# Row sums carried by the neighbour product, and the last block's output product among the first scores

## The chip, the cores and the metric

One Trainium2 chip, of which the kernel uses one core. The metric is the device time of one execution in microseconds (us). TensorE is written PE in the profile (its weight loads PEld), VectorE is DVE, ScalarE is ACT, GpSimd is POOL, and SP issues most DMAs.

## The reference

One layer of a graph network, followed by attention and a mixture of experts, for 4096 tokens of 256 channels, all in float32. Only the first part matters here:

```python
h   = features @ neigh_W.T              # features = layernorm(x) over the 256 channels
deg = adj.sum(axis=1, keepdims=True) + 1.0
h   = adj @ h / deg                     # adj is 4096 x 4096
z   = concatenate([features, h], axis=-1) @ lin_W.T
x   = x + z
```

Then `x = x + ffn(layernorm(x))`, in which `ffn` is causal attention with 4 query heads and 2 key heads of 64 channels, a router to the best 2 of 8 experts, and gated experts. Two facts are used below. A layer-normed row has no gain or offset here, so its 256 channels add up to zero: each channel is minus the sum of the other 255. And `deg` is the row sum of `adj`, which is what `adj` times a column of ones gives.

## The kernel before, in words

**Folding.** `neigh_W` and the second half of `lin_W` are multiplied once at the start into one 256x256 matrix `m_sb` (`fold`, L359 to L367), so the neighbour part is `(adj @ features) @ m / deg`. PE first runs 26 transposes of an identity into an unused bank (`idle`, L657 to L659) and goes on to `fold` when they are done.

**Neighbour product.** The tokens are cut into 8 blocks `b` of 512 rows, and `adj` into 8 x 8 pieces, one 1 MB DMA for each (`load`, L244). `aggregate(b)` (L492) walks over 8 column pieces `jb` and adds each piece's product with the normed features `g[jb]` into four PSUM banks, `acc`. It uses Strassen's scheme: seven products of half size in place of eight. The sums of quarters of `adj` that this needs are made on DVE by `halve` (L448: S1, S2, S4, S3, L459 to L462); the last of them is written in place over a quarter of the piece. The sums of quarters of the features are made once by `halve_x` (L421). Features are normed by `normed_x` (L409, DVE), turned by `turned_x` (L416, PE transposes at L397, ACT copies at L399) and multiplied by the first half of `lin_W` in `features` (L476, PE at L485). All this is done in the first pass, block 0, in between its eight pieces; PE reaches `tr` of block 3 in its second piece.

**Order inside a pass.** The order is written by hand: `steps[jb]` is a list of functions called after the fourth of the seven products of piece `jb`, and `steps[jb, "end"]` after the seventh. In pass `b` (from 1 on) these steps are the query, key and value work of block `b-1` (`qkv`, L580): scales, norm, turn, values, key heads and query heads, at pieces 1 to 6. The heads are rotated by ACT (L638) and POOL (L642, L643). At the end of a pass ACT copies product 1 out of its bank (L522) and DVE adds the seven products up (L523 to L525, L531 to L534) into `neighbours`, which lies in the room of `kT[7]` and `vv[7]`.

**Degrees.** POOL adds the sums S4 and S1 of the eight pieces up into `all_s` (L467 to L474). At the end of the pass PE multiplies `all_s` by ones: four products of 32 columns each, at four column positions of the array (`sums`, L544); ACT copies the result (L550). In the first piece of the next pass PE turns it (`degrees`, L554), DVE adds 1 and inverts it (L556, L559), and `linear` (L561) multiplies `neighbours` by `m_sb` (L566) and adds the result, divided by the degrees, to `res[b]` (DVE, L573). For the last block there is no next pass: `degrees` and `linear` run at once, ahead of attention.

**Attention's start.** Blocks come in `ORDER` 3, 0, 4, 1, 5, 2, 6, 7; the unit of work is a key tile `s` for a pair of heads. `scores` (L792) is 16 PE instructions into one of two double banks (`p_sc0`, `p_sc2`), then an exponential on ACT (L809). `totals` (L818, DVE L829) adds the probabilities up, `values` (L833, PE L843) multiplies them by V. Seven scores are issued ahead of the first values. Other work is placed among the units by number: the first in the list is `last_qkv` (L1150), the query, key and value work of block 7, which reads `res[7]`: statistics on DVE (L159), powers on POOL (L165, L166), norm on DVE (L174), transposes on PE (L1171). DVE runs in program order, so these statistics come after the totals of units 1 to 5.

**PSUM.** In the first part the banks are `g_tr` 0 and 1, `g_pj` 2 and 3, `acc` 4 to 7. In attention `y_third` has 0, `ms` 1, `p_sc1` (`y_first`, `y_second`) 2 and 3, `p_sc0` 4 and 5, `p_sc2` 6 and 7.

Of the kernel before, what the change touches and what calls it, by code (L numbers as in the profile page):

```python
# [9 lines left out]
F32 = mybir.dt.float32  # L10
# [7 lines left out]
P = 128  # L18
# [48 lines left out]
def fast_kernel(  # L67
# [114 lines left out]

    def ratio(pool, b):
# [45 lines left out]
    with (  # L229
# [28 lines left out]
        m_sb = gw.tile([P, 2, C], F32, name="m_sb")  # L258
        l1_sb = qT[6][:, :, 0:C]
        nc.scalar.dma_start(l1_sb, lin_t[0:C, :].rearrange("(c p) o -> p c o", p=P))  # L260
        for n in range(2):
            load_x(1 + n)
            load(n)
# [95 lines left out]
        def fold():  # L359
            for c in range(2):  # L360
                pm = p_pj.tile([P, 512], F32, tag="pj", name=f"pm_{c}")
                for k in range(2):
                    nc.tensor.matmul(
                        pm[:, :C], wn_sb[:, k, c * P : (c + 1) * P], l2_sb[:, k, :],
                        start=(k == 0), stop=(k == 1),
                    )
                nc.scalar.copy(m_sb[:, c, :], pm[:, :C])  # L367
# [53 lines left out]
        def halve_x(b):  # L421

            part = [g[b][:, k] for k in range(7)]
            nc.vector.tensor_sub(part[T1], part[G12], part[G11])
            nc.vector.tensor_sub(part[T3], part[G22], part[G12])
            nc.vector.tensor_sub(part[T2], part[G22], part[T1])
            nc.vector.tensor_sub(part[T4], part[T2], part[G21])
# [13 lines left out]
        neighbours = [  # L441
            kT[NB - 1].rearrange("p (r i) -> p r i", r=2),
            vv[NB - 1].rearrange("p (r t) c -> p r (t c)", r=2),
        ]

        all_s = gs.tile([P, 2, 2, 2 * P], F32, name="all_s")

        def halve(n):  # L448

            if n == NB * NB:  # L450
                return
            a = blocks.pop(n)
            m = {
                f"A{r + 1}{k + 1}": a[:, 2 * k : 2 * k + 2, r * 2 * P : (r + 1) * 2 * P]
                for r in range(2) for k in range(2)
            }
            m["S1"], m["S2"], m["S4"] = sums_at[n % 2]
            m["S3"] = m["A21"]
# [5 lines left out]
            jb = n % NB  # L464
# [71 lines left out]
        def finish(b):  # L536

            made = {}

            def sums():  # L540

                tr = p_tr.tile([P, 2, 2, P], F32, tag="tr", name=f"degT_{b}")
                for t in range(TB):
                    nc.tensor.matmul(  # L544
                        tr[32 * t : 32 * (t + 1), 0, 0, :], ones[:, 0:32],
                        all_s[:, t // 2, 0, t % 2 * P : (t % 2 + 1) * P],
                        start=True, stop=True, skip_group_check=True, tile_position=(0, 32 * t),
                    )
                made["degT"] = gx.tile([P, P], F32, tag="degT", name=f"degs_{b}", bufs=1)
                nc.scalar.copy(made["degT"], tr[:, 0, 0, :])  # L550

            def degrees():
                tr = p_tr.tile([P, 2, 2, P], F32, tag="tr", name=f"deg_{b}")
                nc.tensor.transpose(tr[:, 0, 0, :], made["degT"], ident)  # L554
                deg = made["deg"] = gx.tile([P, TB], F32, tag="deg", name=f"degr_{b}", bufs=1)
                nc.vector.tensor_scalar_add(  # L556
                    deg, tr[:, 0, 0, :].rearrange("p (t i) -> p t i", i=32)[:, :, 0], 1.0
                )
                nc.vector.reciprocal(deg, deg)  # L559

            def linear():  # L561
                for r in range(2):
                    pj = p_pj.tile([P, 2, C], F32, tag="pj", name=f"ph_{b}_{r}")
                    for t in range(2):
                        for c in range(2):
                            nc.tensor.matmul(  # L566
                                pj[:, t, :], neighbours[c][:, r, t * P : (t + 1) * P],
                                m_sb[:, c, :], start=(c == 0), stop=(c == 1),
                            )
                    for t in range(2):  # L570
                        i = 2 * r + t
                        x1 = res[b][:, i, :]
                        nc.vector.scalar_tensor_tensor(  # L573
                            x1, pj[:, t, :], made["deg"][:, i : i + 1], x1,
                            op0=ALU.mult, op1=ALU.add,
                        )

            return sums, degrees, linear

        def qkv(b):  # L580
# [26 lines left out]
            def values_and_logits():  # L607
                for h in range(2):
                    pj = p_pj.tile([P, 2, C], F32, tag="pj", name=f"pv_{b}_{h}")
# [15 lines left out]
            def turned_heads(ms):  # L625
# [21 lines left out]
                [values_and_logits], [lambda: turned_heads((2,))],  # L647
                [lambda: turned_heads((0, 1))],
# [16 lines left out]
        turned_x(0)  # L665
        features(0)
# [21 lines left out]
        for b in range(NB):  # L688
            sums, degrees, linear = finish(b)
# [6 lines left out]
            steps[NB - 1, "end"] = [sums]  # L696
# [8 lines left out]
    with (  # L705
# [8 lines left out]
        p_sc1, p_sc0, p_sc2 = (  # L714
            sc_scope.enter_context(tc.tile_pool(name=f"a_sc{n}", bufs=bufs, space=PSUM))
            for n, bufs in ((1, 2), (0, 1), (2, 1))
# [496 lines left out]


# [1455 lines left out]
```

## Time and profile before

| what | value |
|---|---|
| median of 3 runs | 1541.57 us (1540.42 to 1542.78) |
| the profiled execution, its own time | 1539.6 us |
| its span in the profile | 1537.9 us |
| outside the span | 1.7 us |
| granted PE clock over the span | 0.998 |
| first neighbour product starts | 18.45 us |
| one pass of `aggregate` with its steps (passes 1 to 7) | 60.35 us |
| attention's first score | 525.07 us |
| POOL busy with `all_s`, the form that names `more_sums` | 101.5 us in 72 instructions |

The pass time is the distance of the PE rows of L544 from pass to pass (218.33, 278.68, 339.02, 399.37). A row of a timeline has the start, the length, the engine, the line, the operation, out and in by name, the shape and the number of instructions in it; in brackets stands the idle time of the engine just before, and what ended it. PE's rows overlap by a fraction of a us, [...]so the cost of PE work is read from start to start. A float32 product with 256 columns is two PE instructions and 0.433 us from start to start (8 of them at L514 take 1.73 us).

### The profile page before, as it was taken

The page shows a single profiled execution, that of the slowest core. Times are in us where ns is not written, and L with a number is a line of the kernel's source. Part 1 is how long each engine was busy: PE and PEld are TensorE (multiplying, and loading weights), DVE is VectorE, ACT ScalarE, POOL GpSimd, SP SyncE. Part 2 cuts the span into 40 slices and gives each one's busy share as a digit, 9 for nine tenths or more (in the row PEclk, how much of TensorE's full clock was granted, in tenths as well). Part 3 has the DMA queues.
Part 4 walks back from the last instruction along what each step waited for, and adds up shares of the span by engine and source line. Part 5 has one row for each costly group of instructions (what it writes and reads, how often), then busy time and mean ns, then how long its engine had stood idle before and what let it go on. Part 6 is the DMA issues. An engine that isn't in the chain of part 4 may idle for free.

```text
span 1537.9 us, 28358 instructions
## 1 busy us (share of the span) xinstructions
PE 1524.7 (99%) x10995; PEld 1125.1 (73%) x10995; DVE 1075.4 (70%) x2150; ACT 555.4 (36%) x986; POOL 717.3 (47%) x730
## 2 busy tenths in 40 slices
PE   9999999999999999999999999999999999999998
PEld 7888888888888543444444444458899999999997
DVE  8965655756656467779879879794565777677762
ACT  1101121121120456555656656553122333343331
POOL 3435545554655422364564563442424455455442
PEclk9999999999999999999999999999999999999999
DMA  6334544444445000011010111038766877787855
GB/s 239 128 119 149 174 141 147 151 140 148 153 138 161 22 1 16 29 40 44 33 57 28 34 40 31 28 127 328 225 208 199 263 227 255 240 254 256 270 142 135
DMA packets 69520, 212.16 MB, mean 138 GB/s; under 512 B 17824, under 2 KB 45856, under 8 KB 55744
## 3 DMA queue, kind: packets, MB, share of 16 engines
q1 hardware_dynamic: 56112, 192.25, 36.6%
q0 software_dynamic: 12720, 17.47, 5.7%
q8 instruction: 89, 1.46, 0.4%
q10 hardware_dynamic: 544, 0.52, 0.1%
q14 instruction: 55, 0.45, 0.1%
HBM read 184.48 MB, written 27.13 MB: 138 GB/s over the span
## 4 chain that ended last, share of the span: by engine, by line
PE 94%; DVE 3%; POOL 1%; issue 1%; ACT 1%; DMA 0%; POOLq 0%; DVEq 0%; ACTq 0%
PE acc L514 23%; PE sc L801 15%; PE h L1713 13%; PE y_first L843 5%; PE y_second L843 5%; PE ye_y L1769 5%; PE y_third L843 4%; PE hA L1540 4%; PE ye_y L1670 3%; PE ye_ms L1670 2%; PE pq L629 2%; PE ph L566 2%; PE hD L1540 2%; PE pf L485 1%; PE po L920 1%; PE tx L1428 1%
## 5 line engine op out<-in xcount | busy, mean ns | idle before, releaser
L801 PE MATMUL sc<-qT_all,kT 64*64 64x512 f32 (+3 forms) x2304 | 281.9, 557 | 0.9 <-ACT pt_all L809 0.5
L514 PE MATMUL acc<-a,g 128*128 128x256 f32 x1024 | 245.9, 380 | 0.0
L514 PEld LDWEIGHTS acc<-a,g 128*128 128x128 f32 x1024 | 192.4, 190 | 32.4 <-issue 6.7
L801 PEld LDWEIGHTS sc<-qT_all,kT 64*64 64x64 f32 x2304 | 91.2, 133 | 129.9 <-issue 108.2
L809 ACT ACTIVATE pt_all<-sc 128x1024 f32<-128x1024 f32 (+3 forms) x157 | 149.0, 956 | 95.5 <-PE sc L801 94.9
L469 POOL TENSOR_TENSOR all_s<-all_s,more_sums 128x512 f32<-128x512 f32 x72 | 101.5, 1423 | 120.4 <-DVE more_sums L461 120.4
L1791 POOL DMA_INDIRECT acc_dram<-y,late x40 | 63.2, 1580 | 180.6 <-ACT y L1780 92.4
L514 PE MATMUL acc<-more_sums,g 128*128 128x256 f32 x512 | 126.3, 379 | 0.0
L829 DVE TENSOR_TENSOR late<-late,pt_all 128x1024 f32<-128x1024 f32 (+3 forms) x92 | 106.7, 1160 | 23.1 <-ACT pt_all L809 11.3
L514 PEld LDWEIGHTS acc<-more_sums,g 128*128 128x128 f32 x512 | 97.2, 190 | 13.2
L1713 PE MATMUL h<-late,qT_all 128*128 128x256 f32 (+1 forms) x616 | 105.2, 327 | 0.0
L843 PE MATMUL y_second<-pt_all,vv 64*64 64x512 f32 (+3 forms) x440 | 105.0, 555 | 0.0
L843 PE MATMUL y_first<-pt_all,vv 64*64 64x512 f32 (+3 forms) x440 | 104.3, 553 | 0.0
L1713 PEld LDWEIGHTS h<-late,qT_all 128*128 128x128 f32 x616 | 94.0, 191 | 9.6 <-ACT late L1434 0.8
L399 ACT COPY qT_all<-tr 128x512 f32<-128x512 f32 x30 | 16.2, 589 | 234.7 <-PE tr L397 234.6
L1079 POOL DMA_INDIRECT lists<-row,slots x64 | 89.8, 1402 | 17.9 <-issue 15.2
L638 ACT ACTIVATE rot<-pq 32x512 f32<-32x512 f32 x84 | 49.5, 589 | 120.4 <-DVE kT L636 55.0
L1720 DVE TENSOR_TENSOR late<-si,h 128x256 f32<-128x256 f32 (+2 forms) x87 | 39.9, 467 | 74.4 <-ACT si L1719 43.7
L843 PE MATMUL y_third<-pt_all,vv 64*64 64x512 f32 (+3 forms) x376 | 89.8, 557 | 0.0
L1719 ACT ACTIVATE si<-h 128x256 f32<-128x256 f32 (+2 forms) x87 | 36.5, 421 | 145.1 <-PE h L1713 138.6
L811 POOL TENSOR_SCALAR_AFFINE_SELECT pt_all<-pt_all 128x256 f32<-128x256 f32 x36 | 19.4, 542 | 109.7 <-ACT pt_all L809 82.1
L1713 PE MATMUL h<-late,pt_all 128*128 128x128 f32 (+1 forms) x440 | 65.7, 306 | 0.0
(479 smaller groups left out, 3471.5 us busy)
## 6 DMA issues: line engine op xcount, KB each, us to landing
a<-in_adj_dram SPq DMA_DIRECT2D x64, 1024.0 KB, 5.0
qT_all<-in_w_dram SPq DMA_DIRECT2D x18, 1408.0 KB, 8.4
pt_all<-in_w_dram SPq DMA_DIRECT2D x16, 1408.0 KB, 8.5
res_all<-in_w_dram SPq DMA_DIRECT2D x17, 768.0 KB, 5.1
pt_all<-in_w_dram SPq DMA_DIRECT2D x16, 768.0 KB, 5.0
res_all<-in_w_dram SPq DMA_DIRECT2D x8, 1408.0 KB, 8.2
qT_all<-in_w_dram SPq DMA_DIRECT2D x9, 768.0 KB, 4.4
late<-lists SPq DMA_DIRECT2D x25, 265.0 KB, 2.9
```

Of the source, the lines that this page charges most:

```text
L469: nc.gpsimd.tensor_add(all_s[:, i], all_s[:, i], sums_at[n % 2][k])
L514: nc.tensor.matmul(acc[bank][:, at, :], g[jb][:, right, k, :], m[left][:, k, :], start=(jb == 0 and k == 0 and at == 0), stop=(jb == NB - ...
L801: nc.tensor.matmul(ps[k * HP : (k + 1) * HP, j, :w], kT[sb][hd, i * P + k * HP : i * P + (k + 1) * HP], qT[b][hd, p, off:], start=True, st ...
L809: nc.scalar.activation(pt[:, :, :w], ps[:, :, :w], AF.Exp, scale=HD ** -0.5)
L829: nc.vector.tensor_add(sums[b, p][:, :, off:], before[:, :, off:], pt[:, :, : 512 - off])
L843: nc.tensor.matmul(accs[b, p][k][hd, off:], vv[sb][some, i, hd], pt[some, j, : 512 - off], start=(s == order_of(b)[0]), stop=(s == order_o ...
L1079: put = nc.gpsimd.indirect_dma_start(out=lists[:, :], out_offset=bass.IndirectOffsetOnAxis(ap=chosen[b][:, k, t, :], axis=0), in_=flats[b] ...
L1540: nc.tensor.matmul(bank[:, n, :], m[left][:, c, :], m[right], start=first and n == 0, stop=True, skip_group_check=True,)
L1670: nc.tensor.matmul(p[number], m[left][:, j, :], m[right][:, j, :], start=(n % 4 == 0 and j == 0), stop=(j == 2), skip_group_check=True,)
L1713: nc.tensor.matmul(ps[m % 2][:, m // 2 - q, :], w13_sb[:, c, m * P : (m + 1) * P], xT[:, c, :], start=(c == 0), stop=(c == 1),)
L1769: nc.tensor.matmul(ps[h if last else 0][:, h, :], hT[:, q, cols], w2_sb[:, q, :], start=(q == 0), stop=(q == NF),)
L1791: put = nc.gpsimd.indirect_dma_start(out=(acc_dram if k < NM - LAST else out)[:, :], out_offset=at, in_=y[:, h, :], in_offset=None, comput ...
```

## The change

**Degrees.** After a block's features have been turned and used, ACT writes ones over channel 255 of `g[b]` (in `halve_x`; both token tiles of the quarters G12 and G22). From there on the neighbour product gives the row sum of `adj` in channel 255. The true channel 255 is minus the sum of the others, so its row of `m` is subtracted from the 255 other rows: ACT writes `wn_less` = column 255 of `neigh_W` minus `neigh_W` before `fold`, and `fold` negates when it copies. Row 255 of the new `m_sb` is zero, and it has a 257th column that picks channel 255 out, so `linear` yields 256 outputs and the row sum in one PSUM bank for each token tile. DVE adds 1 and inverts for two tiles at a time. `all_s` with POOL's additions, `sums` and `degrees` are gone. In block 0's start `fold` is cut in two, with `turned_x(0)` between; `idle` has 28 transposes.

**Last block.** `m_sb` is copied by ACT into the room of `qT[7]` (`m_late`), and the two halves of `linear` for block 7 are issued after scores 1 and 2 of attention, into the banks `ms` and `y_first`.

**Places.** The products for values go to the banks of `g_tr`, those of the heads come one piece earlier (keys at piece 4, queries at 5), and `p_sc0` changes places with `p_sc1` in PSUM, so that scores 0, 2, 4 use banks 2 and 3.

```diff
+    m_late = qT_all[:, (NB - 1) * 1024 :][:, 0 : 2 * (C + 1)].rearrange("p (c o) -> p c o", c=2)
+    def linear(pool, b, r, banks, m_sb):
+        for t, ps in enumerate(banks):
+            for c in range(2):
+                nc.tensor.matmul(
+                    ps[:, 0 : C + 1], neighbours[c][:, r, t * P : (t + 1) * P], m_sb[:, c, :],
+                    start=(c == 0), stop=(c == 1),
+                )
+        deg = pool.tile([P, 2], F32, tag="deg", name=f"deg_{b}_{r}")
+        for t, ps in enumerate(banks):
+            nc.vector.tensor_scalar_add(deg[:, t : t + 1], ps[:, C : C + 1], 1.0)
+        nc.vector.reciprocal(deg, deg)
+        for t, ps in enumerate(banks):
+            x1 = res[b][:, 2 * r + t, :]
+            nc.vector.scalar_tensor_tensor(
+                x1, ps[:, 0:C], deg[:, t : t + 1], x1, op0=ALU.mult, op1=ALU.add
+            )
...
-        m_sb = gw.tile([P, 2, C], F32, name="m_sb")
+        m_sb = gw.tile([P, 2, C + 1], F32, name="m_sb")
+        wn_less = kT[0].rearrange("p (c o) -> p c o", c=2)
...
+        def negate_weights():
+            for k in range(2):
+                nc.scalar.activation(
+                    wn_less[:, k, :], wn_sb[:, k, :], AF.Identity,
+                    bias=wn_sb[:, k, C - 1 : C], scale=-1.0,
+                )
+            nc.gpsimd.memset(m_sb[:, 0, C : C + 1], 0.0)
+            nc.gpsimd.tensor_copy(m_sb[:, 1, C : C + 1], ident[:, P - 1 : P])
+        def fold(c):
+            pm = p_pj.tile([P, 512], F32, tag="pj", name=f"pm_{c}")
+            for k in range(2):
+                nc.tensor.matmul(
+                    pm[:, :C], wn_less[:, k, c * P : (c + 1) * P], l2_sb[:, k, :],
+                    start=(k == 0), stop=(k == 1),
+                )
+            nc.scalar.activation(m_sb[:, c, 0:C], pm[:, :C], AF.Copy, scale=-1.0)
...
         def halve_x(b):
+            nc.scalar.copy(
+                g[b][:, 1:4:2, :, HC - 1], ones[:, 0:4].rearrange("p (k t) -> p k t", k=2)
+            )
...
-            for i, k in ((0, 2), (1, 0)):
-                if jb == 1:
-                    nc.gpsimd.tensor_add(all_s[:, i], sums_at[(n - 1) % 2][k], sums_at[n % 2][k])
-                elif jb > 1:
-                    nc.gpsimd.tensor_add(all_s[:, i], all_s[:, i], sums_at[n % 2][k])
-            if jb == NB - 1:
-                ends = all_s[:, :, 0, :]
-                nc.gpsimd.tensor_add(ends, ends, all_s[:, :, 1, :])
-                nc.gpsimd.tensor_add(ends[:, 0], ends[:, 0], ends[:, 1])
-        def finish(b):
...
+        def turn_banks(b, r):
+            return (
+                p_pj.tile([P, 512], F32, tag="pj", name=f"ph_{b}_{r}"),
+                p_tr.tile([P, 2, 2, P], F32, tag="tr", name=f"ph_{b}_{r}_1").rearrange(
+                    "p c t i -> p (c t i)"
+                ),
+            )
...
-                [values_and_logits], [lambda: turned_heads((2,))],
-                [lambda: turned_heads((0, 1))],
+                [values_and_logits, lambda: turned_heads((2,))], [lambda: turned_heads((0, 1))],
...
-        for n in range(26):
+        negate_weights()
+        for n in range(28):
             nc.tensor.transpose(idle[:, n % TB], ident, ident)
-        fold()
+        fold(0)
...
         turned_x(0)
+        fold(1)
         features(0)
...
-            at_end = [degrees, linear]
-        for step in (*behind, *at_end):
-            step()
+            at_end = [lambda b=b: [linear(gx, b, r, turn_banks(b, r), m_sb) for r in range(2)]]
+        nc.scalar.copy(m_late, m_sb)
         load_tables(NB - 1)
...
-        p_sc1, p_sc0, p_sc2 = (
+        p_sc0, p_sc1, p_sc2 = (
...
+        def last_linear(r):
+            linear(ax, NB - 1, r, two_banks(f"ph_{NB - 1}_{r}"), m_late)
...
                 scores(*keys[m])
+                if m in (1, 2):
+                    last_linear(m - 1)
                 if m:
                     totals(*keys[m - 1])
```

More of the change, by code (lines that the diff above doesn't have):

```diff
@@ L181, in fast_kernel @@
     vv = [kvp.tile([P, TB, NKV * HD], F32, name=f"vv{b}") for b in range(NB)]
+    neighbours = [
+        kT[NB - 1].rearrange("p (r i) -> p r i", r=2),
+        vv[NB - 1].rearrange("p (r t) c -> p r (t c)", r=2),
+    ]
+    m_late = qT_all[:, (NB - 1) * 1024 :][:, 0 : 2 * (C + 1)].rearrange("p (c o) -> p c o", c=2)
[15 more added lines that the diff above has]
+            )
     def ratio(pool, b):
@@ L357, in router_wo @@
             )
[L359 to L367, printed above, removed]
+        def negate_weights():
[14 more added lines that the diff above has]
+            nc.scalar.activation(m_sb[:, c, 0:C], pm[:, :C], AF.Copy, scale=-1.0)
         G11, G12, G21, G22, T1, T2, T4 = range(7)
@@ L438, in fast_kernel @@
         ]
[L441 to L446, printed above, removed]
         def halve(n):
@@ L463, in halve @@
             halves_of[n] = m
-            jb = n % NB
-            for i, k in ((0, 2), (1, 0)):
-                if jb == 1:
-                    nc.gpsimd.tensor_add(all_s[:, i], sums_at[(n - 1) % 2][k], sums_at[n % 2][k])
-                elif jb > 1:
-                    nc.gpsimd.tensor_add(all_s[:, i], all_s[:, i], sums_at[n % 2][k])
-            if jb == NB - 1:
-                ends = all_s[:, :, 0, :]
-                nc.gpsimd.tensor_add(ends, ends, all_s[:, :, 1, :])
-                nc.gpsimd.tensor_add(ends[:, 0], ends[:, 0], ends[:, 1])
         def features(b):
@@ L534, in aggregate @@
             nc.vector.tensor_add(neighbours[1][:, 1], u3, p[5])
-        def finish(b):
[L538 to L578, printed above, removed]
+        def turn_banks(b, r):
[5 more added lines that the diff above has]
+            )
         def qkv(b):
@@ L608, in values_and_logits @@
                 for h in range(2):
-                    pj = p_pj.tile([P, 2, C], F32, tag="pj", name=f"pv_{b}_{h}")
+                    pj = p_tr.tile([P, 2, 2, P], F32, tag="tr", name=f"pv_{b}_{h}")
+                    pj = pj.rearrange("p c t i -> p c (t i)")
                     for i in range(2):
@@ L688, in fast_kernel @@
         for b in range(NB):
-            sums, degrees, linear = finish(b)
             if b:
@@ L695, in fast_kernel @@
                     steps[jb + 1] = fs
-            steps[NB - 1, "end"] = [sums]
             aggregate(b, steps)
-            at_end = [degrees, linear]
-        for step in (*behind, *at_end):
-            step()
+            at_end = [lambda b=b: [linear(gx, b, r, turn_banks(b, r), m_sb) for r in range(2)]]
+        nc.scalar.copy(m_late, m_sb)
         load_tables(NB - 1)
@@ L713, in fast_kernel @@
         sc_scope, ctx_h = ExitStack(), ExitStack()
-        p_sc1, p_sc0, p_sc2 = (
+        p_sc0, p_sc1, p_sc2 = (
             sc_scope.enter_context(tc.tile_pool(name=f"a_sc{n}", bufs=bufs, space=PSUM))
-            for n, bufs in ((1, 2), (0, 1), (2, 1))
+            for n, bufs in ((0, 1), (1, 2), (2, 1))
         )
```

## Prediction

> **What bounds the kernel now.** I read the page's engine table first, then PE's timeline at the end of a pass, then the places where PE stood still.
>
> ```profile
> span 1537.9 us, 28358 instructions
> ...
> PE 1524.7 (99%) x10995; PEld 1125.1 (73%) x10995; DVE 1075.4 (70%) x2150; ACT 555.4 (36%) x986; POOL 717.3 (47%) x730
> ```
>
> PE is busy for 99% of the span; only 1537.9 - 1524.7 = 13.2 us are without a matmul. So time can be won in two ways: by taking work from PE, or out of those 13.2 us. POOL's load is half the span, and `all_s` is over 100 us of it, but work taken from POOL is worth only what PE was made to wait for it.
>
> PE at the end of pass 0 (start, length, operation, count):
>
> ```profile
> 96.69 1.03 PE L514 MATMUL acc<-a,g 128*128 128x256 f32 x4
> 97.65 0.43 PE L544 MATMUL degT<-all_s,ones 128*32 128x128 f32 x8
> 98.00 1.99 PE L514 MATMUL acc<-a,g 128*128 128x256 f32 x8
> 99.83 1.03 PE L514 MATMUL acc<-qT_all,g 128*128 128x256 f32 x4
> ...
> 103.29 1.03 PE L514 MATMUL acc<-a,g 128*128 128x256 f32 x4
> 104.15 0.27 PE L554 MATMUL deg<-ident,degs 128*128 128x128 f32 x1
> 104.26 0.60 PE L566 MATMUL ph<-m_sb,kT 128*128 128x256 f32 x2
> 104.69 0.59 PE L566 MATMUL ph<-m_sb,vv 128*128 128x256 f32 x2
> ```
>
> There are no idle times in brackets: PE runs through. Starts give the price. The four instructions of 96.69 take 0.86 us (as from 100.70 to 101.56), so PE is free at 97.55; the eight of 98.00 would take 1.73 and end at 99.83, so they count from 98.10. The degree products (L544) cost 98.10 - 97.55 = 0.55 us. Likewise L554: 103.29 + 0.86 = 104.15, and `ph` counts from 104.69 - 0.43 = 104.26, so 0.105 us.
>
> Next, the waits of PE in the first passes. PE, then DVE:
>
> ```profile
> 30.04 0.41 PE L397 MATMUL tr<-ident,g 128*128 128x128 f32 x2 [0.55 <-DVE g L411]
> 31.22 1.08 PE L397 MATMUL tr<-ident,g 128*128 128x128 f32 x6 [0.77 <-DVE g L411]
> ```
> ```profile
> 20.24 1.38 DVE L411 TENSOR_SCALAR g<-res_all,mv,rstd 128x256 f32<-128x256 f32 x4
> ...
> 28.54 3.27 DVE L411 TENSOR_SCALAR g<-res_all,mv,rstd 128x256 f32<-128x256 f32 x4
> ```
>
> Four norms (L411) take 1.38 us at 20.24 and 3.27 us at 28.54. In between, at 28.14, POOL starts its first `all_s` addition (1.61 us, then one of 1.31 at 29.71). PE wants those norms for the transposes of block 3 and stands for 0.55 + 0.77 = 1.32 us. Later pieces show the same slow norms but no wait.
>
> Last, the passage to attention. PE, then DVE:
>
> ```profile
> 519.10 1.03 PE L514 MATMUL acc<-a,g 128*128 128x256 f32 x4
> ...
> 525.07 1.95 PE L801 MATMUL sc<-qT_all,kT 64*64 64x512 f32 x16
> 527.35 2.00 PE L801 MATMUL sc<-qT_all,kT 64*64 64x512 f32 x16 [0.34 <-ACT late L809]
> ...
> 541.55 0.87 PE L1171 MATMUL tr_l<-ident,h_l 128*128 128x128 f32 x4 [0.28 <-DVE h_l L174]
> ```
> ```profile
> 525.18 0.88 DVE L573 SCALAR_TENSOR_TENSOR res_all<-ph,degr,res_all 128x256 f32<-128x256 f32 x2 [0.85 <-PE ph L566]
> 528.25 6.54 DVE L829 TENSOR_TENSOR late<-late,pt_all 128x1024 f32<-128x1024 f32 x5 [2.19 <-ACT pt_all L809]
> 534.70 1.40 DVE L159 BATCH_NORM_STATS2 st<-res_all 128x6 f32<-128x256 f32 x4
> ...
> 541.09 1.48 DVE L174 TENSOR_SCALAR h_l<-res_all,mv,both 128x256 f32<-128x256 f32 x4 [2.26 <-POOL both L166]
> ```
>
> PE leaves the last neighbour product at 519.10 + 0.86 = 519.97 and starts the first score at 525.07. Its next wait of weight is at 541.55: 0.28 us for `h_l`, which comes down DVE's queue: last result of `linear` (525.18 + 0.88 = 526.06), five totals from 528.25 (6.54 us), statistics from 534.70, two powers on POOL, norm at 541.09. PE and DVE arrive there almost together. This decides what the overlap is worth.
>
> **The change part by part.** The sum is made against the profiled execution (1539.6 us, span 1537.9) and carried to the median, 1541.57; the profiled one is 2.0 us below it, about what runs differ by.
>
> *Degree products, passes 0 to 6.* 7 x (0.55 + 0.105) = 4.6 us of PE. Here the Trainium skill speaks against the change: "TensorE: Matmul & The Clock Gate", section "The mechanism" of its part on row and column tiling, has products at different column positions run side by side, a pack lasting one matmul and some 4 ns for each further tile. Then four strips in two float32 passes cost no more than two passes of 128 columns, 2 x 0.105 and a little: an estimate of 0.24 us in place of 0.55, and 7 x (0.24 + 0.105) = 2.4 us in all. I take the row, because it is this stream's start to start, drain and all, and the seven passes repeat it (157.99, 218.33 and so on in a rhythm of 60.35).
> What is late next? In passes 1 to 6 the next product needs the bank of products 1 and 2, which ACT and DVE empty. In pass 1 DVE's L523 ended only at 158.10 against PE's 157.90, because ACT's copy (157.28) stood behind the rotations of the query heads. Those move one piece (6.9 us) forward, so nothing is late. In pass 0 the next product waits for DVE's L462, which ended at 97.80: 0.3 us of the 0.55 stay. So 4.3 us.
>
> *POOL's additions.* They take no PE time; what they give is the 1.32 us at 30 us: four norms from 28.54 at 1.38 us end at 29.9, and PE, there at 29.5, takes them one by one from 28.9 on. Bounds: 0 (the norms are slow for another cause) and 1.32; I take 1.32, since the 20.24 row is the same operation without POOL. DVE gets faster in other pieces too, for nothing, as PE doesn't wait there.
>
> *Start.* Two more identity transposes: 26 took 6.99 - 1.42 us, so 0.43. `fold` between the transposes and `features` hides the 0.24 us that PE waited for ACT at 10.06. Sum: 0.2 us lost. The two `wn_less` writes are nearest to the `m_sb` copies (0.372 each). PE read `neigh_W` from 6.99 without a wait, so it is there by then; the writes end by about 7.35 and 7.75, PE needs them at 7.54 and 7.97. If they needed a further table load (1.28 us in the one row there is), up to 1 us would be lost; from below, nothing can be won.
>
> *At no cost.* The ones over channel 255 (nearest row: ACT's copy of 128x16, 0.17) lie in ACT's gaps, 4 to 8 us in pass 0; only then does DVE's `halve_x` follow. Without that cover it would be 0.2 us of DVE a piece, against some 1.5 us that DVE has over (8.9 of 10.4). The 257th column: products of 264 columns (L920) take 386 ns, of 256 379, so 1 ns a column, 128 instructions, 0.1 us. Two more adds (0.16) and one inversion (0.18) a pass on DVE, busy 37 of 60.4 us; ACT's copy to `m_late` (near 128x512, 0.59) lies in ACT's 5.46 us of idleness before the first exponential. The heads' earlier place: their banks were read out pieces before, and the pieces of `adj` land 5.0 us after issue, 7.5 us apart, so no DMA is short. SP's queue keeps its order.
>
> *The last block.* Before, PE did 8 x 0.433 = 3.46 us of `linear` in those 5.1 us; then seven scores from 525.07 to 532.72, 7.65 us for 6.06 of work, waiting for ACT's exponentials with only two banks. After, in the old clock: score 0 from 520.1 (banks 2 and 3 are long free); DVE's last additions end at 521.0 (not 522.58, because ACT's copy comes earlier), score 1 from 521.05; `linear` 0 from 522.0 to 523.75; score 2; `linear` 1 from 524.85, when DVE has emptied `ms`, to 526.6; scores 3 to 6 at ACT's pace; first values at 530.8 in place of 532.72. PE has won 1.9 us. But DVE: for `linear` 1 two adds, inversion, two results, from 526.8 to 528.1; then the totals, which now queue behind it, at 528.1 in place of 528.25; statistics at 534.55; `h_l` at 540.95. PE waits 2 us at `tr_l` in place of 0.28, and 0.15 us is left. Bounds: -0.3 (each change between 128- and 64-row products costs 0.1, as from 524.97 to 525.07, and there are more of them) and 1.9. I take 0.15, because DVE's order fixes it.
>
> Sum: 4.3 + 1.32 - 0.2 + 0.15 = 5.6 us: 1539.6 becomes 1534.0, the median 1541.57 becomes 1536.0.
>
> **Rivals.** *The overlap pays in full:* DVE's chain is shorter than I think (POOL's powers at 536.47, 1.07 and 2.07 us, are slow beside DVE and could be faster), and the 1.9 us arrive. Gain 5.6 + 1.75 = 7.3, 1534.3. Against it: the order of DVE's queue. *Removed columns are cheap:* the page's 0.24. Pass 0 then gives nothing; 6 x 0.24 + 7 x 0.105 + 1.27 = 3.45, 1538.1. *The wait at 30 us stays:* 4.3 won, 1537.3. That is also what it means if the change does less than it says: PE's work is gone, but POOL's load did no harm. *Slower:* `m_sb` rows are now 257 floats, so the second half starts at an odd address, and its 32 products (8 blocks, 4 tiles) could stream more slowly. At twice the time 32 x 0.433 = 13.9 us come in: 1541.57 - 5.6 + 13.9 = 1549.9. It decides from 5.6 / 32 = 0.17 us, 40% of a product. No row has an odd start. "SBUF — State Buffer", section "Operand start alignment", allows any multiple of the element size but says that this is about legality, not speed; no run here shows it yet.
>
> **How the numbers follow.** The forecast as worked out 0.55, the overlap in full 0.15, cheap columns 0.13, the wait stays 0.12, slower 0.05. About 0.2% (3.1 us) is what a measurement of this kernel can tell from no change: faster means below 1538.5. That holds for nearly all of the first two, most of the fourth and half of the third: 0.84; within 0.11; slower 0.05. The range, 1533.2 to 1538.8, takes in the four cases on the fast side, and a us of scatter at its lower end; the fifth is left out.
>
> **What would show it.** Passes 1 to 7 at 59.7 us instead of 60.35; no wait at the transposes of block 3, with four norms at 1.4 us; `ph` at 433 ns a product; first values about 2 us sooner after the last neighbour product, and a wait of about 2 us at `tr_l` for `h_l`, with totals starting 8.1 us after that product. I am wrong if passes shorten by less than 0.4 us, if `ph` is longer than 0.45, or if PE doesn't wait at `tr_l`.

## The result

The change makes the kernel faster, by about as much as forecast: 1536.30 us (median of 18 runs, 1533.59 to 1541.07) against 1542.44 us (18 runs, 1538.88 to 1548.33), a ratio of 0.9962 [0.9952, 0.9973]. The forecast was 1536.0. The profiled execution of the changed kernel is its quickest, 1533.59 us, with a span of 1531.7.

The engine table of the page after, PE's line with the span:

```profile
span 1531.7 us, 28057 instructions
...
PE 1519.0 (99%) x10925; PEld 1123.8 (73%) x10925; DVE 1060.9 (69%) x2182; ACT 555.6 (36%) x989; POOL 555.0 (36%) x604
```

PE has lost 5.7 us of work, and 12.7 us without a matmul remain of 13.2: hardly any standing still was won in sum. POOL's load fell from 717.3 to 555.0 us, and nearly all of that was worth nothing, as the experiments show.

The end of pass 0, PE's timeline after:

```profile
95.31 2.75 PE L532 MATMUL acc<-a,g 128*128 128x256 f32 x12
...
101.36 1.03 PE L532 MATMUL acc<-a,g 128*128 128x256 f32 x4
102.22 0.60 PE L193 MATMUL ph<-m_sb,kT 128*128 128x257 f32 x2
102.65 0.60 PE L193 MATMUL ph<-m_sb,vv 128*128 128x257 f32 x2
```

Twelve `acc` instructions run on where the degree products stood between the fourth and the fifth, and `ph` follows the last `acc` at once (101.36 + 0.86 = 102.22). The first of `ph` are 257 columns wide and 0.433 us apart.

The transposes of block 3, PE and then DVE after:

```profile
28.99 1.03 PE L532 MATMUL acc<-a,g 128*128 128x256 f32 x4
29.85 1.08 PE L431 MATMUL tr<-ident,g 128*128 128x128 f32 x8
```
```profile
29.06 1.38 DVE L445 TENSOR_SCALAR g<-res_all,mv,rstd 128x256 f32<-128x256 f32 x4
```

No bracket, eight transposes in one row, and four norms in 1.38 us instead of 3.27.

The passage to attention, PE and then DVE after. The last neighbour product now ends at 513.21 + 0.86 = 514.07 (519.97 before).

```profile
514.17 2.22 PE L782 MATMUL sc<-qT_all,kT 64*64 64x512 f32 x16
...
523.52 2.01 PE L782 MATMUL sc<-qT_all,kT 64*64 64x512 f32 x16 [0.28 <-ACT pt_all L790]
...
535.98 0.76 PE L1152 MATMUL tr_l<-ident,h_l 128*128 128x128 f32 x4 [2.08 <-DVE h_l L174]
```
```profile
522.19 0.48 DVE L203 SCALAR_TENSOR_TENSOR res_all<-y_first,deg,res_all 128x256 f32<-128x256 f32 x1
522.58 6.54 DVE L810 TENSOR_TENSOR late<-late,pt_all 128x1024 f32<-128x1024 f32 x5
529.03 1.40 DVE L159 BATCH_NORM_STATS2 st<-res_all 128x6 f32<-128x256 f32 x4
...
535.43 1.46 DVE L174 TENSOR_SCALAR h_l<-res_all,mv,both 128x256 f32<-128x256 f32 x4 [2.28 <-POOL both L166]
```

The first score starts at once. (By these rows one score is 8 PE instructions, not the 16 that the description of the kernel gives; a row of 16 holds two.) The first values follow at 525.35, 11.28 us after the last neighbour product in place of 12.75. But the totals (L810) stand behind the last result of `linear` (522.19), and PE then waits 2.08 us at `tr_l` instead of 0.28.

By stretches of the two profiled executions (us from start to start):

| stretch | before | after | difference | forecast |
|---|---|---|---|---|
| start to first neighbour product | 18.45 | 18.98 | +0.53 | +0.2 |
| pass 0, to its first `ph` | 85.81 | 83.24 | -2.57 | -1.7 |
| passes 1 to 6, one of them | 60.34 | 59.70 | -0.64 | -0.655 |
| last neighbour product to the score after `tr_l` | 23.03 | 23.25 | +0.22 | -0.15 |
| all that follows | 994.91 | 994.38 | -0.53 | 0 |

The six passes give 3.87, and the sum is 6.2 us. The last line is not the change's: it is made up of -1.1 behind PE's last instruction, +0.5 in the stage of the experts and +0.1 in attention. In the kernels below, whose code in these two stretches is the same, the first takes 6.8 to 8.8 us and the second 314.9 to 324.7. So the experiments are read by stretch, not only by the total.

### The profile page after: what moved, and what is told of

The parts are those of the page before. It is cut to its first block, busy times and chain, and to the rows that moved or that the text cites. A ratio compares the mean times of both kernels' runs of the same rounds, so it can differ in the third digit from the quotient of the medians.

```text
span 1531.7 us, 28057 instructions
## 1 busy us (share of the span) xinstructions
PE 1519.0 (99%) x10925; PEld 1123.8 (73%) x10925; DVE 1060.9 (69%) x2182; ACT 555.6 (36%) x989; POOL 555.0 (36%) x604
## 4 chain that ended last, share of the span: by engine, by line
PE 97%; DVE 2%; POOL 0%; DMA 0%; ACT 0%; issue 0%; SPq 0%; POOLq 0%; DVEq 0%
PE acc L532 25%; PE sc L782 15%; PE h L1697 13%; PE y_first L824 5%; PE y_second L824 5%; PE y_third L824 4%; PE ye_y L1753 4%; PE hA L1524 4%; PE ye_y L1654 3%; PE ye_ms L1654 2%; PE pq L612 2%; PE pf L503 2%; PE hD L1524 2%; PE ph L193 2%; PE po L901 1%; PE tx L1412 1%
## 5 line engine op out<-in xcount | busy, mean ns | idle before, releaser
L810 DVE TENSOR_TENSOR late<-late,pt_all 128x1024 f32<-128x1024 f32 (+3 forms) x92 | 106.7, 1160 | 20.8 <-ACT pt_all L790 8.6
L532 PEld LDWEIGHTS acc<-more_sums,g 128*128 128x128 f32 x512 | 97.2, 190 | 13.2
L625 POOL TENSOR_TENSOR rot<-rot,tables 128x512 f32<-128x512 f32 x21 | 34.2, 1628 | 198.6 <-ACT rot L621 158.4
L532 PE MATMUL acc<-qT_all,g 128*128 128x256 f32 x256 | 65.7, 379 | 0.0
```

The lines of the kernel that those rows point to most:

```text
L532: nc.tensor.matmul(acc[bank][:, at, :], g[jb][:, right, k, :], m[left][:, k, :], start=(jb == 0 and k == 0 and at == 0), stop=(jb == NB - ...
L810: nc.vector.tensor_add(sums[b, p][:, :, off:], before[:, :, off:], pt[:, :, : 512 - off])
```

## The experiments

The theory, after the result: the gain is the degree products on PE and the wait at the third block, and the overlap of `linear` gives nothing because DVE's queue orders the statistics behind the totals. The rivals: the overlap as such helps or hurts; POOL's additions are harmless, and the early wait has another cause; the degree products were cheap, and the move of the heads brought the gain.

### Is the overlap worth anything?

`e1_no_overlap`: the last block's `linear` ahead of attention, as before.

```diff
-        nc.scalar.copy(m_late, m_sb)
+        for f in at_end:
+            f()
...
-                if m in (1, 2):
-                    last_linear(m - 1)
```

> The changed kernel, with the last block's linear issued ahead of attention again (degrees still come in channel 255, m_late is gone). Theory (DVE's queue decides): counted from the start of the last neighbour product's end T, the last result of linear comes at T + 5.3 us, totals start at T + 7.2 (changed kernel: T + 8.5), so the transposes tr_l run at about T + 20.5 in place of T + 21.9, with a wait of PE under 0.6 us in place of 2.1: about 1.4 us faster than the changed kernel. Rival (the overlap with the first scores pays): 1.5 to 3 us slower than the changed kernel, as PE's 3.5 us of linear lie in the open again.

Measured: 1535.08 us, ratio 0.9959 [0.9943, 0.9975]; the join (last neighbour product to the score after `tr_l`) 22.62 us, 0.63 *less* than with the overlap. The rival, by which the overlap saves time, falls. The totals start 7.87 us after the last product (8.51 with the overlap), and the wait at `tr_l` is 0.29 us. It isn't the 1.4 us that I expected, for a reason of its own: score 0 now stands 1.06 us for DVE's `linear` results (L203), because the change gave the first scores banks 2 and 3, which `linear` uses. PE in e1:

```profile
516.68 0.60 PE L193 MATMUL ph<-m_sb,vv 128*128 128x257 f32 x2
518.35 1.95 PE L783 MATMUL sc<-qT_all,kT 64*64 64x512 f32 x16 [1.06 <-DVE res_all L203]
```

`e2_early_stats`: the overlap stays, but the statistics of block 7 are issued ahead of the totals; and `e3_no_overlap_early`: the same without the overlap (the edit of e1, and `scales` called at `m == 1`).

```diff
-                [None, scales], [None, norm],
+                [None], [None, norm],
...
                 if m in (1, 2):
                     last_linear(m - 1)
+                if m == 2:
+                    last_scales()
                 if m:
                     totals(*keys[m - 1])
```

> The changed kernel, with the statistics of block 7 put ahead of the totals of units 1 to 5 in DVE's order. Theory: the chain statistics, powers, norm is what PE waits for at tr_l; with it early, norm ends by T + 19.6 us and PE arrives at T + 19.8, so the wait of 2.1 us goes and the kernel is about 2 us faster than the changed one. Rival (PE's wait is set by the totals, by ACT's exponentials or by the probabilities' rooms): the wait stays or comes back within the next few units, gain under 0.5 us.

> Both edits together: linear of the last block ahead of attention, statistics ahead of the totals. Theory: with DVE's chain out of the way the overlap is worth what PE gains by it, 12.75 - 11.28 = 1.5 us less the degree part before (about 1.2): values start about T + 11.5, tr_l at about T + 20.1 without a wait, so 0.3 us slower than early_stats and 1.8 faster than the changed kernel. Rival (the overlap is worth its full 1.5 us or more once the chain is early): 1.5 us or more slower than early_stats.

Measured: e2's join is 21.09 us, 2.16 less than after's, and e3's 21.86. DVE in e2:

```profile
523.65 9.17 DVE L810 TENSOR_TENSOR late<-late,pt_all 128x1024 f32<-128x1024 f32 x7
532.74 1.47 DVE L174 TENSOR_SCALAR h_l<-res_all,mv,both 128x256 f32<-128x256 f32 x4
```

Seven totals run through, and `h_l` starts at 532.74, 19.20 us after the last product (21.36 after the change). PE comes to `tr_l` and finds it done. So with the banks of the change the overlap is worth 21.86 - 21.09 = 0.77 us (0.3 expected), and the order of DVE's queue decides whether one gets it. But e3 has the wait of e1 at score 0, 1.06 us for banks that the change moved for the overlap's sake. With the first scores in their old banks e3 might lose it: an estimate of 21.86 - 1.06 = 20.80 us, which leaves the overlap nothing. That was not run, so 0.77 is its worth against this e3 only. The totals of time, 1534.93 and 1534.73 us, don't tell these kernels from after: their stage of the experts happened to take 321.0 and 322.0 us in the profiled executions, 316.2 in after's.

### What did POOL's additions cost?

`e4_pool_back`: POOL adds S4 and S1 up again, in all passes, into a tile that nobody reads. `e8_pool_late` does it from pass 1 on (`n >= 8`).

```diff
+            jb = n % NB
+            if n >= 0:
+                for i, k in ((0, 2), (1, 0)):
+                    if jb == 1:
+                        nc.gpsimd.tensor_add(all_s[:, i], sums_at[(n - 1) % 2][k], sums_at[n % 2][k])
+                    elif jb > 1:
+                        nc.gpsimd.tensor_add(all_s[:, i], all_s[:, i], sums_at[n % 2][k])
```

> The changed kernel with POOL's additions into all_s put back in all passes, their result unused (the two additions at a pass's end are left out). Theory: DVE's norms of the second piece become slow again (3.3 us for four in place of 1.4) and PE waits at the transposes of block 3 as before: 1.9 us from start to start, though the profile's idle column shows 1.3; nothing elsewhere. Rival (that wait came from something else, such as the start's order): no wait, 0 us. Second rival (POOL's additions slow DVE everywhere so that passes get longer): passes over 59.7 us.

> The changed kernel with POOL's additions into all_s in passes 1 to 7 only, result unused. Theory: no wait at the transposes of block 3 (29.85 less the start's shift), so first neighbour product to first ph stays 83.24 us as in the changed kernel (85.1 with the additions in all passes). The waits that the additions make in later passes (1.1 us in one pass when they were in all of them) stay: 0 to 1.4 us. Rival (the wait in pass 0 is not from POOL's additions in pass 0): 85.1.

Measured: in e4 pass 0 is 85.14 us, 1.90 longer, with the two brackets of before ([0.55] and [0.77], the norms again in 3.27 us); in e8 it is 83.24. That settles the early wait: it is POOL's, in pass 0, and worth 1.90 us. The brackets show 1.32 of it. From pass 1 on, five passes stay at 59.70 in both kernels and one becomes 61.06 or 61.07: PE waits 1.09 us in e4 for an addition of DVE's (L550), which stands behind the sums of a late piece of `adj`. The changed kernel has that late piece too, without harm: there DVE's last two sums take 0.69 us each, and beside POOL's additions in e4 1.64 and 1.75. No pass of before has that wait, so it belongs to these kernels. In time e4 is at 1541.99 us, ratio 1.0001 [0.9984, 1.0018], and e8, seen once, at 1539.70; of e4's 5.7 us more than after, these two stretches hold 1.90 + 1.36; the rest was not traced.

### What does a pack of column strips cost?

`e5_strips4`: at the end of passes 0 to 6, four products of 32 columns at four column positions, as the degree products were, from constants into an unused bank, and one ACT copy. `e6_strips8`: two such packs.

```diff
+        def strips():
+            tr = p_tr.tile([P, 2, 2, P], F32, tag="tr", name="strips")
+            for n in range(1):
+                for t in range(TB):
+                    nc.tensor.matmul(
+                        tr[32 * t : 32 * (t + 1), 0, n, :], ones[:, 0:32], ident,
+                        start=True, stop=True, skip_group_check=True, tile_position=(0, 32 * t),
+                    )
...
+                steps[NB - 1, "end"] = [strips]
```

> The changed kernel with four products of 32 columns at the four column positions (weights ones, moving an identity, so no wait on data) at the end of passes 0 to 6, and ACT's copy of their bank; the result is unused. It measures the price of the removed degree product by itself. The row of before (0.55 us from start to start): the distance between passes grows from 59.70 to 60.25. Rival (the page's span of a pack, 0.24): 59.94.

> The same with two packs of four one after the other (PE work without use). If the 0.55 us is a fixed cost of changing the tile shape plus one pack of about 0.24: 60.5. If every pack costs 0.55: 60.8.

PE in e5, then in e6, at the end of pass 1:

```profile
155.02 1.03 PE L532 MATMUL acc<-a,g 128*128 128x256 f32 x4
155.97 0.43 PE L558 MATMUL strips<-ident,ones 128*32 128x128 f32 x8
156.33 1.99 PE L532 MATMUL acc<-a,g 128*128 128x256 f32 x8
```
```profile
156.16 0.64 PE L558 MATMUL strips<-ident,ones 128*32 128x128 f32 x16
156.74 1.99 PE L532 MATMUL acc<-a,g 128*128 128x256 f32 x8
```

Passes 1 to 6 take 60.25 us in e5 and 60.47 in e6. The first pack costs 0.55 us and the second 0.22. So both numbers of the prediction are right about something: a further pack costs about what was estimated from the page (0.24), and the group of packs in a stream of full-width products costs 0.33 more, once. By e5's starts 0.09 us of that lies before the pack (155.88 to 155.97) and the other 0.24 behind it. The rival "removed columns are cheap" falls. Times, one run each: 1539.88 and 1543.19 us.

### Is it the products, or the places?

`e7_heads_back`: the heads at the pieces of before, all else as changed. `e12_before_heads`: the kernel before, with only the places changed (products for values in the banks of `g_tr`, heads one piece earlier). The edit of e7:

```diff
-                [values_and_logits, lambda: turned_heads((2,))], [lambda: turned_heads((0, 1))],
+                [values_and_logits], [lambda: turned_heads((2,))],
+                [lambda: turned_heads((0, 1))],
```

> The changed kernel with values, key heads and query heads at pieces 4, 5 and 6 again. Theory: with POOL free of all_s the rotations end early enough, ACT's copy and DVE's first addition are done before the next pass's first product: passes stay at 59.70. Rival (the move is what keeps PE from waiting for that bank, as the prediction had it): 59.9 to 60.0 in passes 1 to 6.

> The kernel before, with only the places changed: values into the banks of g_tr with the key heads at piece 4, query heads at piece 5. Theory: with the degree products at each pass's end PE was not waiting for the first bank, they covered it; passes stay within 0.1 us of 60.34, and the move alone gives nothing but some 1 us at the passage to attention (DVE's last additions come earlier). Rival (the move by itself is a gain of its own, 0.9 us a pass): 59.4 to 59.5.

Both came out far from what I expected. The mean of passes 1 to 6, in us:

| | heads at their old pieces | one piece earlier |
|---|---|---|
| `all_s`, degree products, degrees | 60.34 (before) | 64.27 (e12) |
| none of these | 60.64 (e7) | 59.70 (after) |

Each half alone makes the passes longer; only both together make them shorter. In e7, PE and then ACT at the end of pass 1:

```profile
154.44 1.03 PE L532 MATMUL acc<-a,g 128*128 128x256 f32 x4
156.14 1.99 PE L532 MATMUL acc<-a,g 128*128 128x256 f32 x8 [0.67 <-DVE kT L541]
```
```profile
152.85 2.39 ACT L621 ACTIVATE rot<-pq 32x512 f32<-32x512 f32 x4 [3.65 <-POOL qT_all L626]
155.26 0.37 ACT L540 COPY vv<-acc 128x256 f32<-128x256 f32 x1
```

PE is free at 154.44 + 0.86 = 155.30, and the next product needs the bank that ACT's copy (L540) empties and DVE reads after it. The copy stands behind four rotations of the query heads on ACT. It costs 0.94 us a pass (the eight instructions of 156.14 count from 157.97 - 1.73 = 156.24).

Only a part of this wait was there before, under the cover of the degree products. Before, DVE's first addition (L523) ends at 158.10 and PE is free at 157.90; with the 0.16 us that PE takes after DVE's end in e7 (156.08 to 156.24), that would be 0.36 us. The rest comes from a later copy: it starts 53.61 us after the pass's first `ph` in e7 and 53.02 before, in every one of these passes. POOL's first rotation of the query heads, for which ACT waits, is the cause. POOL and then DVE, before:

```profile
151.88 1.27 POOL L642 TENSOR_TENSOR rot<-rot,tables 128x512 f32<-128x512 f32 x1 [0.55 <-DVE qT_all L460]
151.92 1.78 DVE L461 TENSOR_TENSOR more_sums<-a,qT_all 128x512 f32<-128x512 f32 x1
```

The same two in e7, DVE first:

```profile
149.32 0.69 DVE L491 TENSOR_TENSOR more_sums<-a,qT_all 128x512 f32<-128x512 f32 x1
149.34 1.80 POOL L625 TENSOR_TENSOR rot<-rot,tables 128x512 f32<-128x512 f32 x1 [5.74 <-DVE qT_all L490]
```

Whichever of the two starts first, by 0.02 to 0.04 us, keeps its time, and the other takes 0.5 to 1.1 us longer. By its stretches e7 is 7.5 us longer than after: 5.6 in six passes, and 1.84 in the join (25.08 us), which has another such wait. That is more than the change had won, and its one run, 1541.64 us beside 1539.41 for before, agrees: without the move, the change would have gained nothing.

In e12, PE and then POOL at the end of pass 1:

```profile
157.16 1.03 PE L514 MATMUL acc<-a,g 128*128 128x256 f32 x4
160.71 0.62 PE L544 MATMUL degT<-all_s,ones 128*32 128x128 f32 x8 [2.52 <-POOL all_s L474]
161.25 3.44 PE L514 MATMUL acc<-a,g 128*128 128x256 f32 x8
164.53 1.03 PE L514 MATMUL acc<-qT_all,g 128*128 128x256 f32 x4
```
```profile
155.24 2.95 POOL L469 TENSOR_TENSOR all_s<-all_s,more_sums 128x512 f32<-128x512 f32 x2
158.26 1.26 POOL L473 TENSOR_TENSOR all_s<-all_s 128x512 f32<-128x512 f32 x1
159.60 1.05 POOL L474 TENSOR_TENSOR all_s<-all_s 128x256 f32<-128x256 f32 x1
```

POOL's queue now has the query rotations ahead of the last four additions of `all_s`, which end at 159.60 + 1.05 = 160.65. PE, free at 158.02, stands until 160.71 in front of the degree products. The eight instructions after them take 3.28 us instead of 1.73: the granted clock in that stretch is 0.55. So a pass costs 2.69 + 1.55 = 4.24 us more (64.57 for this one); the six passes, of which the last keeps its clock and takes 62.87, hold 23.5 of the 27.3 us between the spans of e12 (1565.2) and before.

### Which version is best, and what does the wait at `tr_l` really cost?

`e9_after_again` is the changed kernel again, `e10_early_again` is e2 again, `e11_early_loads` is e2 with `neigh_W` first on ACT's queue and the first half of `lin_W` on SP's. They ran beside each other.

```diff
-        nc.sync.dma_start(wn_sb, neigh_w.rearrange("(c p) o -> p c o", p=P))
+        nc.scalar.dma_start(wn_sb, neigh_w.rearrange("(c p) o -> p c o", p=P))
...
-        nc.scalar.dma_start(l1_sb, lin_t[0:C, :].rearrange("(c p) o -> p c o", p=P))
+        nc.sync.dma_start(l1_sb, lin_t[0:C, :].rearrange("(c p) o -> p c o", p=P))
```

> The changed kernel itself once more, as a control on the same chip as the next two. Theory: everything up to attention repeats to 0.1 us (pass 0 83.24, passes 59.70, wait of 1.3 to 2.1 us at tr_l); the stage of the experts differs by some us from run to run of the very same program, as the other kernels suggest. Rival (the experts' stage depends on the edit): it repeats at 316 us. If PE's clock falls to half after the wait, attention is 1.1 to 1.8 us longer than 492.2.

> The kernel with block 7's statistics ahead of the totals, once more. Theory: no wait at tr_l, join 21.1 us in place of 22.5 to 23.3, attention 492.2, no half clock: 2 to 3 us faster than the changed kernel on the same chip. Rival (PE's wait there comes back later): under 0.5 us.

> The same, with neigh_W loaded first on ACT's queue (lin_W's first half goes to SP's in its place), so that the wn_less writes, for which PE waited 0.6 to 1.6 us in the changed kernel, start earlier. Theory: the first neighbour product starts at 18.0 to 18.3 us in place of 18.4 to 19.0, gain 0.3 to 0.7 us. Rival (the loads share the DMA engines, x comes later by what neigh_W comes earlier): no gain, the wait moves to block 0's transposes.

Measured, medians of 5: e9 1534.69 us, ratio 0.9957 [0.9943, 0.9971]; e10 1533.24, 0.9955 [0.9941, 0.9969]; e11 1532.58, 0.9950 [0.9936, 0.9964]. The intervals overlap, so the totals don't rank them, and e10's 2 to 3 us less than e9 did not show (1.45 between the medians); the join sets e9 apart from the other two (23.23, 21.07, 21.08). The earlier load took away the wait of PE for `neigh_W`, yet the first neighbour product came no sooner (18.56 us, 18.47 in e10), and PE waited 0.57 us for a norm of DVE's instead: that idea fails.

The profile of e9 showed what that of after, the quickest of its runs, had not. Two stretches of e9, around the wait at `tr_l` and behind it (the first number after the busy times is the granted clock):

```profile
530.00:536.90 6.90, 4.83 (x48) 1.97 (x44) 4.48 (x12) 2.82 (x5) 4.74 (x5) 1.00 0.00 0
536.90:540.40 3.50, 3.50 (x20) 1.13 (x24) 3.19 (x4) 1.59 (x2) 0.00 (x0) 0.52 0.00 0
```

For 3.4 us after the wait and the transposes, PE runs at half its clock. Attention after that score takes 493.92 us instead of 492.30. The same drop is in e4, e6 and e7, not in after and e5: four of the six profiles that have the 2.08 us wait. Of the eight whose wait there is 1.32 us or less (before, e1, e2, e3, e8, e10, e11, e12) none has it there, and their attention is 492.23 us each time. So the overlap as made costs 0.63 us in the join, and in four of six profiled executions 1.1 to 1.8 us more behind it; with the statistics early it gains 0.77, against the e3 of above.

e8 shows what else sets the wait. It has DVE's order of the changed kernel, but POOL's first power (L166) takes 1.04 us where it takes 2.09 in after, and PE waits 1.32 us instead of 2.08. So the rival about POOL's powers had a point: faster powers shorten the wait, yet the order of DVE's queue alone takes it away.

## Why the prediction was right, and where it was not

**Degree products.** 0.655 us a pass was forecast for passes 1 to 6, and 0.64 came: 59.70 as written. The difference is the 257th column, 16 instructions at some 0.9 ns. e5 confirms the row over the page's estimate.

**"Pass 0 keeps 0.3 us".** It kept nothing: twelve `acc` instructions run through at 95.31. DVE's sum (L462 of before) ends at 96.43 in the changed kernel, 0.26 us after PE passed on to the next piece at 96.17, just as late as forecast. But the first two products of a piece read quarters that need no sum; this one is read by the fourth, at 98.77. I had taken the wrong product as its reader, which the order of products in the code would have told.

**POOL's additions.** The mechanism was right and the term too small: 1.32 us was forecast, 1.90 came, as e4 and e8 show. I added brackets where start-to-start was to be had: PE was free at 28.47 + 0.86 = 29.33, eight transposes take 0.92 us, and the next `acc` came at 32.15, not at 30.25.

**Start.** 0.2 us was forecast lost, 0.53 came in this execution, where the inputs landed later. In ten of the other kernels that begin like the changed one, the first product starts at 18.37 to 18.71 us (before: 18.45). So the term is nil within that scatter. What sets it is the moment at which `wn_less` is written: in after and in those ten the first product follows the first product of `fold` by 11.0 us (11.46 before), and `fold` waits for `wn_less`, up to 7.98 us here and 7.46 in e9. I had `neigh_W` landed by 6.99 and the two writes done by 7.75; here ACT waited for it until 7.42 and took 0.91 for the two.

**The last block.** The reason held: DVE's order, totals 8.51 us after the last product (8.1 forecast) and a wait of 2.08 us. Of the 1.9 us for the first values only 1.47 came, and the join lost 0.22 where I had 0.15 won. What I didn't think of is the clock: I priced a wait of 2 us at its length. In the profiled execution of after that happens to be true; in e9 it cost another 1.6 us.

**"Nothing is late".** The step was right in its outcome, and the price beside it too small. I named a lag of 0.2 us (158.10 against 157.90) as what the heads' move had to cover; without the move it is 0.94 a pass. PE's start after DVE's end makes 0.36 of the 0.2, and the other 0.6 is POOL's rotation, which loses its start to DVE once `all_s` is gone. I had taken the other queues' times from before, as if the change did not touch them.

**The odd start of `m_sb`'s second half.** It costs nothing: a `ph` product takes 434 ns on average (seven from 102.22 to the row at 105.26) against 433, and the difference is no more than what the column costs. The slower rival falls. "The wait at 30 us stays" falls with pass 0. "The overlap pays in full" falls as the change stands, and e2 shows where its time was: in the order of DVE's queue.

The sum came out at 5.6 forecast and 6.1 in the medians. That it came so near is in part luck: the terms that were off mostly cancelled. Pass 0 gave 0.9 us more, and the join 0.4 less, with the half clock behind it in some executions.

## What to carry to other kernels

A step that fills time on the bottleneck engine may be covering a wait: before counting it as gain, redo the arrival times without it, on every queue that feeds the next instruction. Two edits that each move a queue can be worth less than nothing alone and pay together, so price them as a pair. Engines that slow each other belong to these queues: here 0.02 us decided which of two kept its time. Where work is pulled forward on one engine, look at which in-order queue holds the consumer's operand, and move that entry too.

## What was not expected of the hardware

**A wait of 2 us can halve PE's clock, if it falls well.** The traces hold the moments at which the granted clock changed. In each of the 14, all of them lie a whole number of 3.413 us behind the first rise (4.3 to 7.2 us), and each of the nine halvings inside a kernel lasted 3.41 us. So the clock is decided window by window. The windows around the wait, in e9 and then in after (length, PE's busy time; the granted clock is again the first number after the busy times):

```profile
533.45:536.86 3.41, 1.42 (x12) 0.89 (x16) 1.92 (x7) 0.59 (x1) 1.64 (x4) 1.00 0.00 0
536.86:540.27 3.41, 3.41 (x20) 1.05 (x24) 3.10 (x4) 1.61 (x2) 0.00 (x0) 0.50 0.00 0
```
```profile
532.02:535.44 3.42, 1.88 (x20) 0.46 (x12) 1.14 (x2) 1.42 (x2) 3.27 (x4) 1.00 0.00 0
535.44:538.85 3.41, 2.87 (x24) 1.48 (x28) 3.27 (x8) 1.49 (x3) 0.34 (x1) 1.00 0.00 0
```

In e9 the wait lies within one window, in after a border cuts it. In all 14 traces every such window at full clock with up to 1.42 us of PE's rows is followed by a half clock, and none with 1.47 us or more (e4, near its end) is. e12 fits: five passes with 0.82 to 1.40 us in the window of the wait, the sixth, which keeps its clock, with 1.69. An estimate from these figures: a wait must bring some 3.41 - 1.42 = 2.0 us into one window, so 1.32 us can't do it alone, and 2.08 us does it in some executions only.

The Trainium skill, "TensorE: Matmul & The Clock Gate", section "What's actually happening", puts the drop after an idle window of about 3.4 us that runs free of the kernel. Length and free running agree with the traces; but the window need not be idle, as 1.42 us of work in it did not save the clock. Its section on the PE-mode transpose says that transposes don't count as busy in the same way. Here the traces say otherwise: the clock rises at 6.37 us in after, when PE has run nothing but transposes (the first other product starts at 7.98), and without them e5's window from 538.25 has 1.03 us and kept its clock, while one of e12 with 1.40 us, in which there are none, lost it.

**A group of column strips has a price of its own** among full-width products: 0.33 us, paid once, more than the 0.22 of a pack. That the change of the tile shape makes it is likely; no run changed the shape alone.

**One stage scatters by itself.** The experts' stage, whose code is the same in all these kernels, took 314.9 to 324.7 us in the profiled executions (from the first product into `hA`, 1195.98 us in after, to the first of `ye_ms` from `qT_all`, 1512.13), and in two executions of the changed kernel 316.2 and 317.8. Most of the difference is PE standing still, 0.0 us in all in e11 and 7.4 in e4, each time up to 1.3 us for ACT or DVE. Why they are late was not tried. Attention, where the clock stays full, repeats to 0.1 us in all but one (e5, which waited 1.2 us for weights at its end).
